# Turning a feed-forward pair with 64x64 identity products on the quarters of the array in place of 128x128 transposes

## The chip, the core and the metric

The kernel runs on one core of a Trainium2 chip. The metric is the device time of one execution in microseconds. Besides it there is a profile of one execution, with the start and the length of every instruction on TensorE (PE, with its weight loads as PEld), VectorE (DVE), ScalarE (ACT), GpSimd (POOL) and of the DMA queue of SyncE (SP).

## The reference, cut to what matters

Layer 0 works on `x` of four batches, 512 time steps, 128 x 64 features; layer 1 is a filter over time by Fourier modes. All is float32. The change sits where layer 0 ends, in the store of its output:

```python
to = layernorm(jnp.swapaxes(to, 1, 2), time_ln_g, time_ln_b)
x = x + to.reshape(b, t, f, h)
mid = jax.nn.gelu(x @ ffn_W1 + ffn_b1)      # 64 -> 256
x = x + (mid @ ffn_W2 + ffn_b2)             # 256 -> 64
...
x = _L1_conv_ref(x, w_real, w_imag)         # layer 1
```

## The kernel before

Layer 0 keeps the data feature-major: a chunk is 128 features (two groups of 64) on the partitions and 512 times along the free axis. 64 chunks make one batch; they are worked in 32 pairs. Layer 1 reads the data time-major from DRAM (`x4`), so each pair has to be turned before it is stored. In every second pair the two groups of 64 stand exchanged (the list HALVES does this on the host).

The stages of layer 0 are generators that a hand-written order (`in_turn`) advances by shares, two at a time; TensorE's order is exactly the order in which they issue (`tc.manual_schedule`). The other engines' queues are filled by a planner, which places each instruction by the times that it works out itself, except where `keep_in_program_order` pins it. The stages are: `project` (L412, keys, values and receptance), `scan`, `attend_and_convolve`, `convolve_time` with its taps (L632 on ScalarE, L636 on VectorE) and sums (`add_up`, L250), `open_feed`, and `feed_forward`. A part of the next batch's time convolution is made ahead inside `feed_forward` of batches 0 and 1 (`convolve_ahead`; `normed` gives L624 and L627 on VectorE, `tapped` gives L632 and L636).

`feed_forward` of batches 0 and 1 stands beside `project` of batches 2 and 3, that of batch 2 beside `convolve_time` of batch 3, that of batch 3 alone. I call them passes 0 to 3. Pass by pass, for each pair:

- `store` turns the pair finished one or two pairs before: eight transposes (L781) into one of two PSUM pairs of banks, `m` and `c`, which `unit()` hands out in turn. ScalarE copies the banks to `ob`, in pairs of even number with one instruction (L794), in pairs of odd number with two, which set the exchanged groups right (L789). Behind the second of these a GpSimd DMA writes `ob` (L790).
- `widen` is issued four times (L745: four products of 64x64 weights, one on each quarter of the array, each in two passes), each time into the next bank pair of `unit()`; ScalarE makes the gelu, `mid` (L750).
- `narrow` comes after each `widen` (L760) and sums in two further banks; after the fourth, VectorE adds the residual (L773) and makes `x4t`.
- `residual` (L704, L705 on VectorE) and `add_residual` (L713 on ScalarE, L716 on VectorE) prepare the pair after the next.

So one block of TensorE is: project or sums if any, turn, then widen and narrow four times by turns. The lines that set a float32 turn are:

```python
pt = unit()
for j, x4t in enumerate(x4s.pop(i)):
    for t in range(NT):
        nc.tensor.transpose(pt[:, j, t * P : (t + 1) * P], x4t[:, t * P : (t + 1) * P], ident)
```

Of the kernel before, what the change touches and what calls it, by code (L numbers as in the profile page):

```python
# [16 lines left out]
P = 128  # L17
T = 512
NF = 128
H = 64  # L20
# [5 lines left out]
NT = T // P  # L26
# [54 lines left out]
def layer0(ctx, tc, dram, x, xt, vecs, wkvr, wo, wdec, wconv, fbias, w1, fb1, w2, fb2, x4):  # L81
# [4 lines left out]
    nc = tc.nc  # L86
# [19 lines left out]
    def two(pool, tag):  # L106
        return pool.tile([P, 2, SL], F32, tag=tag, name=tag)


    ident = const.tile([P, P], F32, name="ident")  # L110
# [51 lines left out]
    halves = [slice(0, H), slice(H, P)]  # L162
# [133 lines left out]
    def spare(tag, n):  # L296
        if tag in ("wk", "wx"):
            return wxp.tile([P, 2, n], F32, tag=tag, name=tag, bufs=2 if tag == "wk" else 3)
        return fr.tile([P, 2, n], F32, tag=tag, name=tag, bufs=4 if tag == "z" else 3)

    def c_bank():
        return two(ps_c, "c")
# [4 lines left out]
    def of_p():  # L307
        return ps_p.tile([P, SL], F32, tag="p", name="p")
# [336 lines left out]
    def convolve_ahead(b, bank):  # L645


        rb, mb = yield from rows(bank, *carried[b], "rm3")
        ahead[b] = rb, mb
        for i in range(AHEAD):  # L650
            xr = spare("x1", SL)
            normed(b, i, xr, xr, rb, mb, True)
            yield
            tapped(b, i, xr, spare("z", SL), True)
            yield
# [43 lines left out]
    def residual(b, i):  # L699
        rb, mb = scale[b]  # L700
        x2 = fetch("kx", x2d, b, i)
        to = fetch("kh", tod, b, i)
        d = two(bk, "kd")
        nc.vector.tensor_tensor(d, to, pair_of(rb), ALU.mult)  # L704
        nc.vector.tensor_tensor(d, d, pair_of(mb), ALU.subtract)  # L705
        return x2, d

    def add_residual(b, i, x2, d):
        x3 = spare("z", SL) if b == B - 1 and i < 2 else bk.tile([P, 2, SL], F32, tag="k3", name="x3", bufs=3)
        for j in range(2):  # L710
            c = slice(2 * i + j, 2 * i + j + 1)

            tc.keep_in_program_order(nc.scalar.activation(  # L713
                d[:, j, :], d[:, j, :], AF.Identity, bias=vec[:, B4, c], scale=vec[:, G4, c]
            ))
        nc.vector.tensor_tensor(x3, d, x2, ALU.add)  # L716
        return x3
# [9 lines left out]
    def feed_forward(b):  # L727
        x3s = opened.pop(b)
        mids, x4s, obs, sums2 = {}, {}, {}, {}
        lag = 1 if b + 2 < B else 2  # L730
        turn = [0]
        while not free_s[0]:
            yield BLOCKED
        feeding[0] = True

        def unit():
            turn[0] ^= 1
            return two(ps_m, "m") if turn[0] else c_bank()

        def widen(i, q):  # L740
            x3 = x3s[i]
            pm = unit()
            for h in range(2):
                for j in range(2):
                    nc.tensor.matmul(  # L745
                        pm[halves[j], h, :], lhsT=w1_sb[halves[h], q * H : (q + 1) * H], rhs=x3[halves[h], j, :],
                        start=True, stop=True,
                    )
            mid = mids[i, q] = bk.tile([P, 2, SL], F32, tag="mid", name="mid", bufs=4)
            gelu = nc.scalar.activation(mid, pm, AF.Gelu_apprx_tanh, bias=fb1_sb[:, q : q + 1])  # L750
            if i == NPR - 3:
                after["scalar"] = gelu.ins

        def narrow(i, q):
            if q == 0:
                sums2[i] = of_p(), ps_s.tile([P, SL], F32, tag="s", name="pb")
            mid = mids.pop((i, q))
            for h in range(2):
                for j in range(2):
                    nc.tensor.matmul(  # L760
                        sums2[i][j][halves[h], :], lhsT=w2_sb[halves[j], q, :], rhs=mid[halves[j], h, :],
                        start=q == 0, stop=q == 3,
                    )
            if q < 3:
                return
            x3 = x3s.pop(i)
            if lag > 1:
                pair = spare("wx", SL)
                x4s[i] = [pair[:, j, :] for j in range(2)]
            else:  # L770
                x4s[i] = [bk.tile([P, SL], F32, tag="x4t", name="x4t", bufs=3) for _ in range(2)]
            for j, pa in enumerate(sums2.pop(i)):
                summed = nc.vector.scalar_tensor_tensor(x4s[i][j], pa, fb2_sb, x3[:, j, :], ALU.add, ALU.add)  # L773
            if i == NPR - 3:
                after["vector"] = summed.ins

        def store(i):
            pt = unit()
            for j, x4t in enumerate(x4s.pop(i)):
                for t in range(NT):  # L780
                    nc.tensor.transpose(pt[:, j, t * P : (t + 1) * P], x4t[:, t * P : (t + 1) * P], ident)  # L781
            s = i // 2
            if i % 2 == 0:
                obs[s] = bk.tile([P, NT, SL], F32, tag="ob", name="ob")
            o = obs[s][:, :, i % 2 * 2 * P : (i % 2 + 1) * 2 * P].rearrange("p t (j w) -> p j t w", j=2)
            pt = pt.rearrange("p j (t w) -> p j t w", t=NT)
            if i % 2:
                for h in range(2):
                    nc.scalar.copy(o[:, :, :, halves[1 - h]], pt[:, :, :, halves[h]])  # L789
                nc.gpsimd.dma_start(  # L790
                    x4[b][:, s * SL : (s + 1) * SL].rearrange("(t p) d -> p t d", p=P), obs.pop(s)
                )
            else:
                nc.scalar.copy(o, pt)  # L794

        early = None
        done = 0.0
        quarter = 2.25 * (NPR + 1) / (NPR + lag)
        widen(0, 0)
        widen(0, 1)  # L800
        for i in range(NPR + lag):
            if i >= lag:
                store(i - lag)
            for q in range(4):
                done += quarter
                if i < NPR:
                    if q < 2:
                        widen(i, q + 2)
                    elif i + 1 < NPR:
                        widen(i + 1, q - 2)  # L810
                    if i + 2 < NPR and q == 1:
                        coming = residual(b, i + 2)
                        if b == B - 1 and i % 4 == 2:
                            after["sync"].append(last_fetch[0].ins)
                    if i + 2 < NPR and q == 3:
                        x3s[i + 2] = add_residual(b, i + 2, *coming)
                    narrow(i, q)
                if q == 3 and b + 2 < B and i > 1:
                    early = early or convolve_ahead(b + 1, lambda: unit()[:, 0, :])
                    next(early, None)  # L820
                if q == 3 or narrowly:
                    yield done
                    done = 0.0
        feeding[0] = False
# [400 lines left out]
```

## Time and profile before

| | |
|---|---|
| time, median of 3 runs | 3683.86 us (3683.42 to 3687.7) |
| the profiled execution | 3685.27 us |
| its span, first to last instruction | 3683.5 us |
| mean granted TensorE clock | 0.985 |
| busy: PE, PEld, DVE, ACT, POOL | 94%, 37%, 73%, 48%, 12% |
| L781, all turns | 1024 transposes, 133.7 us of PE |
| pass 0, 820 to 1200 us | PE 97%, DVE 73%, ACT 63% |
| pass 1, 1470 to 1850 us | PE 97%, DVE 73%, ACT 63% |
| pass 2, 2110 to 2450 us | PE 91%, DVE 91%, ACT 84% |
| pass 3, 2450 to 2722 us | PE 98%, DVE 60%, ACT 80% |
| layer 1, from 2722 us | PE 96% |

A row of a timeline gives the start in us from the span's start, the length in us, the engine, the line, the operation, what it writes and reads, the shape, and how many instructions were joined. The bracket at its end is the idle time of the engine ahead of it and what ended that. A row of the waits names the waiting engine and line, whom it waited for, and us in total, times, and the longest. Float32 products show as two passes each, transposes as one. PE's ends are modelled, its starts are not.

### The profile page before, as it was taken

Reading aid. Unit: us, or ns where it says so; the run is one execution under the profiler, and the core shown is the slowest. Engines: PE = TensorE matmul, PEld = TensorE weight load, DVE = VectorE, ACT = ScalarE, POOL = GpSimd, SP = SyncE. Lnnn points to the kernel's source line nnn. Section 1 sums busy time; section 2 is a strip of 40 time slices with the busy share of each in tenths; the row PEclk is TensorE's granted clock in tenths of the full one; section 3 lists DMA queues with packets and bytes.
Section 4 is the critical chain, followed back from the end, with each engine's and each line's share of the span. In section 5 each row is a group of like instructions: output and inputs, shape, how many; then the busy total and the mean of one; then the engine's idle time right before and its main releaser. Section 6 shows DMA issues by size and latency. Waiting matters only on the chain. (4 is left out here: it accounts for less than half of the span.)

```text
span 3683.5 us, 54528 instructions
## 1 busy us (share of the span) xinstructions
PE 3480.4 (94%) x20553; PEld 1372.7 (37%) x20553; DVE 2671.6 (73%) x3498; ACT 1778.1 (48%) x2331; POOL 448.4 (12%) x657
## 2 busy tenths in 40 slices
PE   8989998889999899999999989999999999999998
PEld 3433332224333223443322333333333833328433
DVE  4464469986777896677789799956677277892677
ACT  0013346556666565666656588878864200152100
POOL 0000012220111121011112121200000000001000
PEclk9999999999999999999999999999999999999999
DMA  9886647787885688888568777746668478994687
GB/s 302 284 269 211 204 164 269 255 277 264 294 288 183 237 279 280 277 289 292 172 239 284 239 238 256 238 173 218 225 194 277 154 245 293 308 290 161 209 298 261
DMA packets 427991, 910.58 MB, mean 247 GB/s; under 512 B 32976, under 2 KB 83920, under 8 KB 423632
## 3 DMA queue, kind: packets, MB, share of 16 engines
q1 hardware_dynamic: 354160, 637.18, 53.1%
q0 software_dynamic: 71680, 268.46, 20.3%
q8 instruction: 164, 2.69, 0.3%
q10 hardware_dynamic: 1888, 1.45, 0.1%
q14 instruction: 99, 0.81, 0.1%
HBM read 638.46 MB, written 268.50 MB: 246 GB/s over the span
## 5 line engine op out<-in xcount | busy, mean ns | idle before, releaser
L760 PE MATMUL p<-mid,w_sb 64*64 64x512 f32 x2048 | 549.3, 595 | 17.9 <-DVE wx L773 17.9
L760 PE MATMUL pb<-mid,w_sb 64*64 64x512 f32 x2048 | 533.2, 595 | 0.0
L750 ACT ACTIVATE mid<-m,fb_sb 128x1024 f32<-128x1024 f32 x256 | 284.8, 1113 | 93.0 <-PE m L745 91.6
L750 ACT ACTIVATE mid<-c,fb_sb 128x1024 f32<-128x1024 f32 x256 | 284.5, 1111 | 91.2 <-PE c L745 89.1
L745 PE MATMUL m<-x,w_sb 64*64 64x512 f32 x2016 | 283.3, 613 | 7.5 <-ACT ob L794 5.3
L745 PE MATMUL c<-x,w_sb 64*64 64x512 f32 x2016 | 276.9, 604 | 12.9 <-ACT mid L750 6.6
L760 PEld LDWEIGHTS p<-mid,w_sb 64*64 64x64 f32 x2048 | 153.7, 134 | 290.9 <-issue 261.0
L1071 ACT COPY two<-a 128x512 f32<-128x512 f32 x64 | 37.5, 586 | 426.3 <-PE a L1066 426.3
L412 PE MATMUL a<-xp,wx 128*128 128x512 f32 x512 | 235.2, 603 | 0.5 <-DVE me L267 0.5
L1094 PE MATMUL b<-xin,avg_sb 128*128 128x512 f32 x512 | 230.8, 593 | 3.3 <-DVE xin L1100 3.3
L1100 DVE TENSOR_TENSOR xin<-b,pm 128x512 f32<-128x512 f32 x256 | 159.0, 683 | 97.9 <-PE b L1097 82.9
L581 ACT ACTIVATE sq<-x 128x1024 f32<-128x1024 f32 x128 | 135.1, 1055 | 150.5 <-DVE x L576 150.4
L250 PE MATMUL st<-x,ones 128*32 128x512 f32 x512 | 183.9, 609 | 23.8 <-DVE x L576 23.7
L636 DVE SCALAR_TENSOR_TENSOR to<-kd,vec,to 128x511 f32<-128x511 f32 (+1 forms) x272 | 197.0, 743 | 11.5 <-ACT to L632 8.0
L713 ACT ACTIVATE kd<-kd,vec 128x512 f32<-128x512 f32 x256 | 192.7, 803 | 3.1 <-DVE kd L705 3.1
L538 DVE TENSOR_TENSOR x<-a,xp 128x1024 f32<-128x1024 f32 x128 | 156.1, 1219 | 48.1 <-PE a L534 45.5
L946 DVE COPY xf<-b 128x256 f32<-128x256 f32 x128 | 54.4, 425 | 178.9 <-PE b L1040 170.0
L636 DVE SCALAR_TENSOR_TENSOR z<-x,vec,z 128x511 f32<-128x511 f32 x240 | 175.6, 744 | 5.0 <-ACT z L632 3.6
L716 DVE TENSOR_TENSOR x<-kd,kx 128x1024 f32<-128x1024 f32 x126 | 154.0, 1223 | 33.5 <-ACT kd L713 33.5
L534 PE MATMUL a<-rst,wo_sb 64*64 64x512 f32 x1024 | 143.3, 630 | 27.4 <-DVE x L538 25.3
L773 DVE SCALAR_TENSOR_TENSOR x4t<-p,fb_sb,x 128x512 f32<-128x512 f32 x64 | 47.7, 746 | 160.0 <-PE pb L760 157.5
L704 DVE TENSOR_TENSOR kd<-kh,rm 128x1024 f32<-128x1024 f32 x128 | 155.6, 1219 | 6.8 <-ACT rm L284 4.6
(271 smaller groups left out, 6762.7 us busy)
## 6 DMA issues: line engine op xcount, KB each, us to landing
xp<-in_xt SPq DMA_DIRECT2D x256, 512.0 KB
kh<-to SPq DMA_DIRECT2D x156, 512.0 KB
x<-x POOLq DMA_DIRECT2D x128, 512.0 KB, 4.6
kx<-x SPq DMA_DIRECT2D x128, 512.0 KB
x<-ob POOLq DMA_DIRECT2D x64, 1024.0 KB, 8.1
xin<-x SPq DMA_DIRECT2D x64, 1024.0 KB
out<-xin POOLq DMA_DIRECT2D x64, 1024.0 KB, 6.3
x<-x SPq DMA_DIRECT2D x96, 512.0 KB
```

The costliest lines, as they stand in the source:

```text
L250: nc.tensor.matmul(st[32 * q : 32 * q + 32, :], lhsT=ones, rhs=src[:, j, :], start=first, stop=last,)
L412: nc.tensor.matmul(pa[:, k, :], lhsT=wq[:, j, k * P : (k + 1) * P], rhs=xp[:, j, :], start=first and j == 0, stop=last and j == 1,)
L538: nc.vector.tensor_tensor(x1, at, xp, ALU.add)
L636: tap = nc.vector.scalar_tensor_tensor(to[:, j, k:], xr[:, j, : SL - k], vec[:, w, c], to[:, j, k:], ALU.mult, ALU.add)
L704: nc.vector.tensor_tensor(d, to, pair_of(rb), ALU.mult)
L713: tc.keep_in_program_order(nc.scalar.activation(d[:, j, :], d[:, j, :], AF.Identity, bias=vec[:, B4, c], scale=vec[:, G4, c]))
L716: nc.vector.tensor_tensor(x3, d, x2, ALU.add)
L745: nc.tensor.matmul(pm[halves[j], h, :], lhsT=w1_sb[halves[h], q * H : (q + 1) * H], rhs=x3[halves[h], j, :], start=True, stop=True,)
L750: gelu = nc.scalar.activation(mid, pm, AF.Gelu_apprx_tanh, bias=fb1_sb[:, q : q + 1])
L760: nc.tensor.matmul(sums2[i][j][halves[h], :], lhsT=w2_sb[halves[j], q, :], rhs=mid[halves[j], h, :], start=q == 0, stop=q == 3,)
L1094: nc.tensor.matmul(po[j], lhsT=avg_sb[:, j, :], rhs=xin[:, j, :], start=True, stop=False)
L1100: nc.vector.tensor_tensor(by_n(xin[:, j, :]), by_n(po[j]), by_c(pm[j % 2][:, j // 2, :]), ALU.add)
```

## The change

The eight transposes of a pair become 32 products. Of each 128 x 128 square of `x4t`, the four 64 x 64 quarters are loaded as weights, each on the quarter of the array that its rows (features) and its output partitions (times) name, and multiplied by the 64 x 64 identity, which moves through. The feature halves go to two banks: bank `h` holds rows `h` of both chunks. The copies read the banks in that new order; in pairs of odd number each of the two copies now reads one bank alone.

```diff
         def store(i):
             pt = unit()
+            pt = pt.rearrange("p h (t j w) -> p h t j w", t=NT, j=2)
             for j, x4t in enumerate(x4s.pop(i)):
                 for t in range(NT):
-                    nc.tensor.transpose(pt[:, j, t * P : (t + 1) * P], x4t[:, t * P : (t + 1) * P], ident)
+                    for h, rows in enumerate(halves):
+                        for k, at in enumerate(halves):
+                            tt = slice(t * P + k * H, t * P + (k + 1) * H)
+                            nc.tensor.matmul(
+                                pt[at, h, t, j, :], lhsT=x4t[rows, tt], rhs=ident[rows, rows], start=True, stop=True
+                            )
             s = i // 2
             if i % 2 == 0:
                 obs[s] = bk.tile([P, NT, SL], F32, tag="ob", name="ob")
-            o = obs[s][:, :, i % 2 * 2 * P : (i % 2 + 1) * 2 * P].rearrange("p t (j w) -> p j t w", j=2)
-            pt = pt.rearrange("p j (t w) -> p j t w", t=NT)
-            if i % 2:
+            o = obs[s][:, :, i % 2 * 2 * P : (i % 2 + 1) * 2 * P].rearrange("p t (j h w) -> p h t j w", j=2, h=2)
+            if i % 2 == 0:
+                nc.scalar.copy(o, pt)
+            else:
                 for h in range(2):
-                    nc.scalar.copy(o[:, :, :, halves[1 - h]], pt[:, :, :, halves[h]])
+                    nc.scalar.copy(o[:, 1 - h], pt[:, h])
                 nc.gpsimd.dma_start(
                     x4[b][:, s * SL : (s + 1) * SL].rearrange("(t p) d -> p t d", p=P), obs.pop(s)
                 )
-            else:
-                nc.scalar.copy(o, pt)
```

## The prediction

> **What bounds the kernel now.** I first read the busy shares: TensorE 94% of 3683.5 us, VectorE 73%, ScalarE 48%. The cheap conclusion, "TensorE bounds it, so a cheaper turn is a gain", needs a check by stage, because `store` runs only in the four feed-forward passes. The table of stretches gives them: passes 0 and 1 (820 to 1200 and 1470 to 1850 us) have TensorE busy 97%; pass 2 (2110 to 2450 us) is at 91% on TensorE and 91% on VectorE; pass 3 (2450 to 2722 us) at 98% on TensorE. A pass works in blocks, one per pair of feature chunks: TensorE issues other work (projection L412 in passes 0 and 1, sums L250 in pass 2, nothing in pass 3), then the turn L781, then four times widen (L745) and narrow (L760). The turn fills one of the bank pairs m and c. Widen 1 takes the other, widen 2 needs the turn's pair back (ScalarE's copy, L794 or L789), widen 3 needs the gelu of widen 1 (L750, "mid").
>
> So in each pass I look at what widens 2 and 3 wait for. The timelines of ScalarE and TensorE in a block of pass 0, times in us from the span's start, duration, then the wait:
>
> ```profile
> 984.31 1.04 PE L781 MATMUL m<-ident,x4t 128*128 128x128 f32 x8
> ...
> 985.27 1.09 PE L745 MATMUL c<-x,w_sb 64*64 64x512 f32 x8
> 985.38 1.01 ACT L794 COPY ob<-m 128x1024 f32<-128x1024 f32 x1 [2.75 <-PE m L781]
> ...
> 987.38 0.81 ACT L632 ACTIVATE z<-x,vec 128x512 f32<-128x512 f32 x1 [0.98 <-DVE x L627]
> ...
> 988.10 1.09 ACT L750 ACTIVATE mid<-c,fb_sb 128x1024 f32<-128x1024 f32 x1
> ...
> 989.10 0.81 ACT L632 ACTIVATE z<-x,vec 128x512 f32<-128x512 f32 x1
> ...
> 989.25 1.09 PE L745 MATMUL c<-x,w_sb 64*64 64x512 f32 x8 [0.31 <-ACT mid L750]
> ```
>
> ScalarE's gelu of widen 1 was ready to run at 986.4, but stands behind a tap activation (L632) that waits for VectorE; it ends at 989.19, and widen 3 starts 0.05 later. That 0.31 us is TensorE's only wait in the block, and it comes 9 times in each of passes 0 and 1.
>
> The waits of TensorE in pass 2, and two stretches of it (TensorE, weight loads, VectorE, ScalarE, GpSimd busy):
>
> ```profile
> PE p L760 <- DVE wx L773: 17.9, 6, 5.9
> PE c L745 <- ACT ob L789: 6.3, 11, 0.6
> PE m L745 <- ACT ob L794: 4.6, 9, 0.6
> ...
> 2160.00:2180.00 20.00, 18.95 (x165) 6.54 (x168) 19.79 (x23) 18.26 (x22) 3.64 (x5) 1.00 0.81 278
> ...
> 2280.00:2300.00 20.00, 18.95 (x168) 6.46 (x164) 19.83 (x23) 18.25 (x22) 3.99 (x5) 1.00 0.83 265
> ```
>
> Here VectorE is 99% busy, and in 20 blocks widen 2 already waits about 0.5 us for the turn's copy; about every fifth block TensorE waits some 2 us for VectorE.
>
> Pass 3, TensorE, its weight loads and ScalarE:
>
> ```profile
> 2573.76 1.09 PE L781 MATMUL m<-ident,wx 128*128 128x128 f32 x8
> 2574.78 1.09 PE L745 MATMUL c<-x,w_sb 64*64 64x512 f32 x8
> ...
> 2576.57 0.21 PEld L745 LDWEIGHTS m<-x,w_sb 64*64 64x64 f32 x8 [0.72 <-ACT ob L794]
> ...
> 2574.11 1.51 ACT L713 ACTIVATE kd<-kd,vec 128x512 f32<-128x512 f32 x2
> 2575.52 0.99 ACT L794 COPY ob<-m 128x1024 f32<-128x1024 f32 x1
> ```
>
> The copy stands behind two L713, these behind the gelu of widen 4. It ends at 2576.51, widen 2 starts 0.05 us later. So pass 3, though TensorE shows 98%, runs on a loop: widen 4, gelu, two L713, copy, widen 2. The turn is not in it.
>
> **What the Trainium skill says.** TensorEngine Tiling, Key Properties: changing the tiling mode drains TensorE. The trace agrees: from the last pass of L760 (0.43 us long) to L781 and from L781 to L745 about 0.1 us is lost each time (2565.05+0.43 to 2565.58; turns start to start 0.109, yet eight of them and the way to L745 take 0.96), and the first pass of L745 takes 0.05 more (1.09 against 1.04). TensorE: Matmul & The Clock Gate, LDWEIGHTS: a load is charged by its columns, so 64 cost half of 128; no row shows a steady run of them on four quarters. The same page, "Wait — 56ns, not 53.3ns?": starts never come closer than about 25 ns, however small the product; the trace starts passes on different quarters 0.01 apart, so this is only my upper bound. The same page, Architectural detail: ScalarE and VectorE are strict FIFO; the two fences above on passes 0 and 3 show just that.
>
> **The change part by part.** (a) Per turn, 8 transposes in one pass each (starts 0.109 us apart) go, and 32 products in two passes each come: 64 passes, 16 rounds if four quarters run at once, as L745 does (8 passes of 0.43 in 0.86). A round is bounded below by 64 moving columns, 64/512 of 0.43, or 0.054. The nearest row is L194, 64x64 weights with 16 columns on two quarters: four rounds in 0.41 us, of which 0.21 is the last one's length, so 0.20/3.1, about 0.06. I take 0.06: 0.96 us a turn; ends 0.90 (0.056 a round) and, as an estimate from the page's 25 ns a pass, 1.6.
> (b) The drains. By the product ahead, in the order of the trace, there are 126 runs of turns (two of them of two turns). 56 follow 128-row products (L412 and few others): before 0.96+0.05, after 0.09+0.96, so +0.04. 43 follow L760: before 0.11+1.02+0.05, after 0.96, so -0.22. 27 follow L250 (another mode): -0.13. If all of it counted: 56x0.04 - 43x0.22 - 27x0.13 = -11 us. But it doesn't: some 30 of the 43 lie in pass 3, whose loop leaves the turn out: 0. The 27 are in pass 2, where widen 2 waits for ScalarE anyway: 0, but for some five at its end. In passes 0 and 1 only the blocks with no wait count, about 34 x 0.04 = +1.4. The dozen mode changes at the ends of passes give -2. Sum of (a) and (b): -1.
> (c) The copies (L794: one of 1.0 us; L789: two of 0.59). L794 now writes runs of 64 where it wrote 128; L789 already did, and pays 586 ns for 512 columns, as the plain copy L1071 does (586). So 0; at most 0.05 x 64, outside pass 3 hidden. Their DMA (L790) is the same; two are issued two GpSimd instructions later, with 24 us to spare: 0. 0.9 MB more instructions to fetch beside 910 MB: 0.
> (d) **What moves.** ScalarE's order isn't written by hand; a planner places it, and I compared the orders of the two built programs. In passes 0 and 1, 18 blocks had copy, L632, gelu, L632, gelu; now copy, L632, L632, gelu, gelu. Four blocks had L632, copy, L632, gelu; now both L632 stand ahead of the copy. In pass 2 nearly every block's second L632 goes from behind the copy to before it. VectorE, GpSimd and SP keep their orders, but for seven L636 one place earlier and four GpSimd exchanges; TensorE's own is fixed. An L632 in the row costs ScalarE 0.72 us (987.38 to 988.10).
> Passes 0 and 1: the first L632 still starts at 987.38 (it waits for VectorE, whose chain starts at the end of the last narrow, not at the turn). The second now takes 988.10 to 988.81, the gelu ends 989.90 rather than 989.19, widen 3 starts 0.71 later. Behind the waiting L632 stand four gelus and two L713 on ScalarE; widen 3 waits for the first gelu, and narrow 3 behind it. Narrows and widens follow in order on TensorE, with no later wait to give it back, and the next block's VectorE chain starts from that narrow. In the four other blocks the copy and widen 2 come 0.71 later. 22 x 0.71 = +15.6.
> Pass 2: the loop gelu 4, L713, L713, L632, square, copy, widen 2 takes 9.8 us and grows by 0.71 in about 20 blocks; VectorE needs 10.0 in those, and some 2 us a cycle of five blocks is TensorE's wait for VectorE. So of 5 x 0.71 = 3.5 a cycle some 2 are absorbed; 1.5 x 4.6 cycles: +7. Ends: 0 and 24 x 0.71 = 17.
> Sum: -1 + 15.6 + 7 = +21.6. Against the profiled execution (3685.27 us; its span 3683.5 and 1.8 around it) that is 3706.9; against the median of 3683.86, 1.4 lower, 3705.5. I say **3705**.
>
> **Rivals.** *The drain pays* (faster): the L632 are covered after all, because the waits of L745 in passes 0 and 1 don't lengthen, and the full -11 of (b) comes: 3673. For it: some 110 drains go (two at each of the 43, one at each of the 27). Against: ScalarE's order is fixed and 0.05 us separates its ends from the starts of widens 2 and 3. It decides where an added wait is under 0.5 us in each of 22 blocks. 7%. *Cancelled*: part of the 15.6 is given back at the ends of passes 0 and 1 (there TensorE waits 1.9 us for a GpSimd power, L232, and 8.5 for L773) and pass 2 absorbs all: about 3689. 10%. *Quarters don't pack* (slower still): 1.6 us a turn; +0.6 in 34 blocks of passes 0 and 1, and +0.4 x 32 in pass 3, where the slack of the loop is then used up: +33 more, 3738. Against: L745 and L760 pack fully. 10%. The rest, 73%, is my forecast. That the change doesn't do what it says (transposes kept) is excluded by the built program, which has 4096 products of 64x64 and no transpose.
>
> **How the numbers follow.** A measurement of this kernel can tell about 0.2%, 7.4 us, from no change: 3676.5 to 3691.2. The forecast's own ends: pass 2 at 0 gives 3698, at 17 gives 3715. The range 3689 to 3722 takes in the cancelled case's middle and half of looser packing, and leaves out some 2 in 10. Faster 0.07, same 0.10, slower 0.83.
>
> **What would show it.** In the profile after: L632, L632, L750 in a row in passes 0 and 1, and the wait of L745 for mid 1.0 us in place of 0.31, 9 times a pass; pass 2 with waits for the copies near 1.2 us; pass 3 as long as before, with TensorE's wait ahead of widen 2 grown by 0.2; turns of 0.96 us. If pass 3 is shorter by 7 us, (b) is wrong; if passes 0 and 1 are not 7 to 8 us longer each, (d) is.

## The result and the profile after

| | before | after |
|---|---|---|
| time, median of 4 runs | 3683.64 us (3679.46 to 3687.7) | 3700.74 us (3695.82 to 3703.18) |
| span of the profiled execution | 3683.5 us | 3697.5 us (3699.32 in all) |
| TensorE busy | 3480.4 us | 3470.3 us |
| ScalarE's copies of the turns, mean | 1002 and 584 ns | 1002 and 584 ns |

The kernel became slower: ratio 1.0036, 95% interval 1.0021 to 1.0051. TensorE is busy 10 us less and the kernel takes 17 us more by the medians (8 to 19 by the interval).

Where the time lies is read best from ScalarE's copies of the even blocks, 16 in a pass, one fixed point in every second block. From the start of the first to the start of the last of a pass (us):

| | pass 0 | pass 1 | pass 2 | pass 3 |
|---|---|---|---|---|
| before | 364.3 | 362.7 | 316.5 | 242.1 |
| after | 369.9 | 370.0 | 320.7 | 241.7 |
| difference | +5.6 | +7.3 | +4.3 | -0.3 |

Together +16.9, about the difference of the medians. The other stretches (start-up, ends of passes, layer 1) differ by up to 13 us from kernel to kernel in the profiles of this study without following the edit, so they are left alone.

Two of the differences need a caution, because single profiles also differ in TensorE's granted clock. The trace shows it halved in stretches of 3.4 us. In pass 0 the profile before has two such stretches, at 1140 and 1168 us; pass 1, and both passes of the kernel after, have one each. The one at 1140 is the additional one, and it costs 1.6 us: the span between two even copies in which it lies takes 26.68 us in pass 0 and 25.08 in pass 1. Without it pass 0 grew by 7.2. Pass 2 is taken up again below.

The turn first. Line numbers after: L781 is now L785, L794 is L793, L789 is L796; lines up to L776 keep theirs. TensorE's timeline in a block of pass 3 of the kernel after:

```profile
2585.09 1.11 PE L785 MATMUL m<-ident,wx 64*64 64x64 f32 x64
2586.03 1.04 PE L745 MATMUL c<-x,w_sb 64*64 64x512 f32 x8
...
2587.33 0.60 PE L760 MATMUL pb<-mid,w_sb 64*64 64x512 f32 x2
2588.02 1.09 PE L745 MATMUL m<-x,w_sb 64*64 64x512 f32 x8
```

The turn of 64 passes takes 0.94 us up to the start of widen 1, which follows with no gap; its row is 1.04 long, not 1.09. At the end of the excerpt, widen 2 starts 0.69 us after the last row of the narrow ahead of it (2587.33 to 2588.02). Ahead of the later widens of the block the same distance is 0.42. The difference of 0.27 us is the wait for the copy, and the one place where TensorE stands still in the block.

Now ScalarE's timeline in a block of pass 0, the kernel after:

```profile
1009.56 1.01 ACT L793 COPY ob<-m 128x1024 f32<-128x1024 f32 x1 [3.00 <-PE m L785]
1011.31 1.52 ACT L632 ACTIVATE z<-x,vec 128x512 f32<-128x512 f32 x2 [0.73 <-DVE x L627]
1012.73 1.09 ACT L750 ACTIVATE mid<-c,fb_sb 128x1024 f32<-128x1024 f32 x1
```

and TensorE's in the same block:

```profile
1009.31 1.04 PE L745 MATMUL c<-x,w_sb 64*64 64x512 f32 x8
...
1013.88 1.09 PE L745 MATMUL c<-x,w_sb 64*64 64x512 f32 x8 [0.95 <-ACT mid L750]
```

The two L632 now stand in a row ahead of the first gelu, which ends 4.5 us after widen 1 began, where it was 3.9 before; widen 3 waits 0.95 us in place of 0.31. The waits of TensorE in one round of pass 0 (870 to 1140 us), after:

```profile
PE c L745 <- ACT mid L750: 8.4, 9, 1.0
PE m L745 <- ACT ob L793: 1.6, 2, 0.8
```

They were 2.6 and 0.4 us before. One more wait changed: once in each of passes 0 and 1 TensorE waits for a GpSimd power (L232), 1.9 us before and 1.2 after. And in pass 2 (2120 to 2465 us), after:

```profile
PE p L760 <- DVE wx L773: 16.0, 9, 5.8
PE c L745 <- ACT ob L796: 12.8, 11, 1.6
PE m L745 <- ACT ob L793: 9.6, 9, 1.4
```

Widen 2's waits for the copies, 6.3 and 4.6 before, have doubled; the wait for VectorE's sums fell only from 17.9 to 16.0. The granted clock changed as well. These are pass 2 of the kernel before, one of its stretches at half clock, and pass 2 of the kernel after; the third number from the end is the granted clock:

```profile
2136.00:2453.00 317.00, 291.69 (x2416) 110.52 (x2416) 285.50 (x324) 267.16 (x315) 59.71 (x77) 0.97 0.71 238
2259.90:2263.30 3.40, 3.40 (x22) 1.91 (x18) 3.40 (x5) 0.53 (x1) 0.00 (x0) 0.50 0.99 348
2145.00:2466.00 321.00, 288.20 (x4096) 112.29 (x4096) 284.92 (x323) 267.79 (x313) 74.80 (x77) 0.98 0.69 235
```

Before, the clock was halved for 20.5 us of pass 2, in stretches of which four begin about 1 us after the end of a wait of 1.9 to 2.2 us for L773, and 10.2 us of clock were lost. After, it was halved for 10.2 us, and 5.1 were lost.

### The profile page after: what moved, and what is told of

Its sections match the earlier page's. It is cut to its first block, busy times and chain, and to the rows that moved or that the text cites. A ratio compares the mean times of both kernels' runs of the same rounds, so it can differ in the third digit from the quotient of the medians.

```text
span 3697.5 us, 68871 instructions
## 1 busy us (share of the span) xinstructions
PE 3470.3 (94%) x27721; PEld 1384.9 (37%) x27721; DVE 2673.9 (72%) x3498; ACT 1777.9 (48%) x2331; POOL 462.9 (13%) x657
## 5 line engine op out<-in xcount | busy, mean ns | idle before, releaser
L760 PE MATMUL p<-mid,w_sb 64*64 64x512 f32 x2048 | 548.4, 594 | 16.0 <-DVE wx L773 16.0
L760 PE MATMUL pb<-mid,w_sb 64*64 64x512 f32 x2048 | 532.0, 594 | 0.0
L745 PE MATMUL c<-x,w_sb 64*64 64x512 f32 x2016 | 272.7, 598 | 32.2 <-ACT mid L750 17.3
L745 PE MATMUL m<-x,w_sb 64*64 64x512 f32 x2016 | 276.6, 604 | 16.0 <-ACT ob L793 12.9
L760 PEld LDWEIGHTS p<-mid,w_sb 64*64 64x64 f32 x2048 | 154.1, 134 | 284.4 <-issue 237.8
L412 PE MATMUL a<-xp,wx 128*128 128x512 f32 x512 | 236.3, 605 | 0.5 <-DVE me L267 0.5
L250 PE MATMUL st<-x,ones 128*32 128x512 f32 x512 | 183.7, 610 | 26.1 <-DVE x L576 26.0
L713 ACT ACTIVATE kd<-kd,vec 128x512 f32<-128x512 f32 x256 | 192.6, 802 | 3.1 <-DVE kd L705 3.1
L773 DVE SCALAR_TENSOR_TENSOR x4t<-p,fb_sb,x 128x512 f32<-128x512 f32 x64 | 48.0, 749 | 170.0 <-PE pb L760 167.4
L704 DVE TENSOR_TENSOR kd<-kh,rm 128x1024 f32<-128x1024 f32 x128 | 155.7, 1219 | 9.5 <-ACT rm L284 5.3
```

The source lines that it names most:

```text
L250: nc.tensor.matmul(st[32 * q : 32 * q + 32, :], lhsT=ones, rhs=src[:, j, :], start=first, stop=last,)
L412: nc.tensor.matmul(pa[:, k, :], lhsT=wq[:, j, k * P : (k + 1) * P], rhs=xp[:, j, :], start=first and j == 0, stop=last and j == 1,)
L713: tc.keep_in_program_order(nc.scalar.activation(d[:, j, :], d[:, j, :], AF.Identity, bias=vec[:, B4, c], scale=vec[:, G4, c]))
L745: nc.tensor.matmul(pm[halves[j], h, :], lhsT=w1_sb[halves[h], q * H : (q + 1) * H], rhs=x3[halves[h], j, :], start=True, stop=True,)
L760: nc.tensor.matmul(sums2[i][j][halves[h], :], lhsT=w2_sb[halves[j], q, :], rhs=mid[halves[j], h, :], start=q == 0, stop=q == 3,)
```

## The experiments

Two theories. **Order**: the loss is where the planner put the L632 on ScalarE, and the turn itself is worth next to nothing where it now stands. **Turn**: the products, their drains or the re-shaped copies cost the time. Each kernel's lines are shifted by its edit; the tile names tell which is which. The ratios are to the kernel before, measured beside each run.

### Products, old order

```diff
+    def order(z, ins):
+        follow(z, ins)
+    def placed(j, z, ahead_of):
+        if ahead_of is not None:
+            if j and ahead_of < 11:
+                order(z, copies[-1] if ahead_of in (3, 7) else gelus[-4])
+            return
...
+        if k in (9, 15, 21, 26):
+            order(z, gelus[-8])
+        elif j == 1 and k > 2:
+            order(z, copies[-1] if k in (7, 8, 13, 14, 19, 20, 24, 25, 30, 31) else copies[-2])
```

`follow` adds an edge of order alone between two instructions of ScalarE; `gelus` and `copies` hold those traced so far, `k` counts the taps of pass 2.

> The kernel after, with each second L632 activation pinned to the place on ScalarE that it has in the kernel before (behind the first gelu of its block in passes 0 and 1, behind the copy in pass 2), nothing else. Theory 1, the order is the loss: the +7.6, +7.6 and +4.4 us by which passes 0, 1 and 2 are longer in the kernel after go, so about 3701 - 19 = 3682 us, and L745 waits for mid near 0.3 us in pass 0 in place of 1.0. Theory 2, the turn itself is the loss (its products, their drains, or the form of the copy): the time stays at 3700 us, and the waits of L745 stay near 1.0.

Measured: 1.0001 of the kernel before (0.9991 to 1.0011); passes 363.1, 362.8, 316.0 and 241.7 us. (The expectation read the three differences as 7.6, 7.6 and 4.4; those of the table above are used here.) TensorE's wait for mid in pass 0, this run:

```profile
PE c L772 <- ACT mid L777: 2.0, 9, 0.2
```

The whole loss goes with the order. In the trace ScalarE's 2331 instructions stand in the order of the kernel before, without exception, and GpSimd's 657 in that of the kernel after; so GpSimd's few exchanges are not the cause. The same run says that the products, in the old order, gain nothing that the time shows.

Pass 2 is less certain than passes 0 and 1. Four of the runs below also have the products and the old order in pass 2, and it takes 317.3 to 318.4 us there. Two others (the turn twice, and the first try at pass 3) have the products and the new order: 318.7 and 318.8. The kernel after, with 320.7, is the longest of its kind, and this run the shortest of its own. By the means the order costs 2.1 us in pass 2, with 0.3 to 4.7 between single profiles. Passes 0 and 1 of these kernels repeat within 0.4 us where the order is the same.

### Transposes, new order

The same places, with the edge turned round (`follow(ins, z)`), on the kernel before.

> The kernel before, with its 128x128 transposes, and ScalarE's order of the kernel after (gelu or copy pinned behind the L632 activation that comes ahead of it there). Theory 1, the order is the loss: 3684 + 19 = 3703 us, with L745 waiting 1.0 us for mid 9 times in pass 0. Theory 2, the turn itself: 3684 us. In between, near 3693: the order hurts only together with the other turn.

Measured: 1.0049 (1.0037 to 1.0061); passes 369.2, 369.6, 319.1 and 242.0. TensorE's wait for mid in pass 0:

```profile
PE c L773 <- ACT mid L778: 7.9, 8, 1.0
```

The loss comes without the products (ScalarE's order is here that of the kernel after, but for one gelu). The theory of the turn falls, from both sides.

### Products, both L632 behind the second gelu

```diff
-            if j and ahead_of < 11:
-                order(z, copies[-1] if ahead_of in (3, 7) else gelus[-4])
+            if ahead_of < 11:
+                order(z, gelus[-3])
```

> Products with the old order in pass 2, and in passes 0 and 1 both L632 of a pair in a row again, but behind the second gelu of the block in place of ahead of the first. If it is the run of two (1.4 us against a slack of some 0.4 to 0.7) that delays a gelu, passes 0 and 1 are again about 370 us each and the whole 3687 + 14 = 3701 us, with TensorE waiting near 1.0 us for mid at another gelu. If it is the place right behind the copy that has no slack, passes 0 and 1 are near 363 us and the whole near 3687.

Measured: 0.9970 (0.9962 to 0.9977); passes 0 and 1 take 357.5 us each, better than before. ScalarE in a block of pass 0 of this run:

```profile
983.39 1.01 ACT L821 COPY ob<-m 128x1024 f32<-128x1024 f32 x1 [3.00 <-PE m L813]
984.31 1.11 ACT L777 ACTIVATE mid<-c,fb_sb 128x1024 f32<-128x1024 f32 x1
986.03 1.11 ACT L777 ACTIVATE mid<-m,fb_sb 128x1024 f32<-128x1024 f32 x1 [0.60 <-PE m L772]
987.04 1.51 ACT L657 ACTIVATE z<-x,vec 128x512 f32<-128x512 f32 x2
988.45 1.10 ACT L777 ACTIVATE mid<-c,fb_sb 128x1024 f32<-128x1024 f32 x1
```

The run of two does no harm here: no widen waits for a gelu any more, but for one of 0.5 us at the end of each pass. By then VectorE's L627 has long been done, so the 0.73 us of idle ScalarE goes as well, and the third gelu starts 2.42 us after the second, where the second followed the first after 1.72, without making TensorE wait. So it is not that two stand in a row but that they stand ahead of the first gelu, where one of them already cost a wait.

The gain is larger than either expectation, because a wait costs TensorE more than its row shows. In the old order the row gives 0.2 us, yet a pair of blocks with one such wait takes 23.61 us there and 23.18 here. The narrow ahead of widen 3 takes 1.23 us from its start to widen 3's in place of 0.86, and widen 3 itself 0.91 in place of 0.86: together 0.43. The idle time in a row is counted only from the modelled end of the product ahead (0.60 us after its start, where the next one follows after 0.43 if nothing holds it).

### The turn twice in pass 3

```diff
-                            nc.tensor.matmul(
+                            for _ in range(2 if b == B - 1 else 1):
+                                nc.tensor.matmul(
```

> The kernel after, with every one of the 64 products of a turn issued twice in pass 3 (the second overwrites the first with the same values), which makes 32 turns of 0.96 us about 0.9 us longer each. If the turn lies beside the loop in pass 3 (it ends 0.9 us before the copy that follows it can start, because ScalarE still has the two L713 to do), pass 3 stays at 241.7 us within 2 us and the wait of the second widen for the copy stays near 1.0. If the turn is on the loop, pass 3 grows by 30 x 0.9 = 27 us, to 3728 us in all.

Measured: 1.0082 (1.0069 to 1.0094); pass 3 260.8 us, +19.0, neither of the two. A block grew from 8.15 to 8.75 us, by 0.60, for a turn longer by 0.95. TensorE and ScalarE in a block of pass 3 of this run (the other 5 of the turn's 128 passes stand in rows of their own):

```profile
2598.35 2.08 PE L786 MATMUL c<-ident,wx 64*64 64x64 f32 x123
```

```profile
2598.93 1.51 ACT L713 ACTIVATE kd<-kd,vec 128x512 f32<-128x512 f32 x2
2600.58 1.07 ACT L798 COPY ob<-c 128x512 f32<-128x512 f32 x2
```

The turn now ends together with the two L713 (2600.43 and 2600.44), and the copy follows both. The first 0.35 us of the added turn are hidden, the rest shows: TensorE's own time in a block, without waits, is 4 x 1.716 + 0.94 = 7.80, and 7.80 + 0.95 = 8.75. The turn lay beside the loop, but only 0.35 us below it. My "1.0 us of wait" was misread. It is this row of TensorE's weight loads, in the kernel after:

```profile
2588.01 0.21 PEld L745 LDWEIGHTS m<-x,w_sb 64*64 64x64 f32 x8 [0.97 <-ACT ob L793]
```

The loads wait while TensorE still works on the narrow ahead; of the 0.97 us TensorE stood idle 0.27 (the timeline of pass 3 above), and 0.05 went into the longer row of the widen behind the wait.

### Pass 3 with the L713 elsewhere: four failures, then two that worked

The first try placed one L713 behind the second and one behind the third gelu, and fetched a block earlier.

```diff
+                    if apart and i + 2 < NPR and q in (1, 2):
+                        half_residual(i + 2, coming[1], q - 1)
+                        if q == 2:
+                            x3s[i + 2] = add_residual(b, i + 2, *coming, True)
+                            if i + 3 < NPR:
+                                coming = residual(b, i + 3)
```

> The kernel after; in pass 3 alone the two L713 activations of a block, which stand between its fourth gelu and the next copy, are placed one after the second and one after the third gelu, where ScalarE is idle 0.6 us each, and their operands are fetched a block earlier. If pass 3 is a loop in which the copy waits for gelu 4 and two L713, and the second widen waits for the copy (1.0 us of wait in each of 28 blocks), the wait nearly goes: 28 x 0.9 = -25, about 3676 us. If pass 3 is held by something else as well (the gelus, the fetches), under 5 us are gained: 3696 to 3701.

> The kernel before with the same move of the L713 in pass 3. Loop theory: the wait of 0.8 us in each of some 26 to 30 blocks goes, -20, about 3663 us. The turn of products is 0.2 us a turn shorter with what lies around it, and this was hidden in pass 3: if so, pass 3 of the run before this one (products, halves early) is about 6 us shorter than pass 3 of this run; if the products' turn is no shorter on TensorE's path, the two passes are equal.

Measured: 1.0275 (1.0262 to 1.0289) and 1.0238 (1.0225 to 1.0252); pass 3 326.3 and 324.9 us. Then the addition of the residual was pinned behind the sums traced ahead of it, and ScalarE's old order was put back in passes 0 to 2 of the products:

```diff
+        if halves_done:
+            tc.keep_in_program_order(whole)
```

> Products with ScalarE's old order in passes 0 to 2, and in pass 3 the two L713 early as before, with one thing mended: the addition of the residual is pinned on VectorE behind the two sums of the block before, which it overtook in the first try and held up (DVE waited 155.7 us for L710 in pass 3, and the sums came late). If the loop theory of pass 3 holds (copy behind gelu 4 and two L713, second widen behind the copy), the 28 waits of 1.0 us go to about 0.1: -25 against the products with the old order, 3688 - 25 = 3663 us. If another loop is as long (the gelus' own, VectorE's, the fetches), pass 3 stays near 241.7 us and the time near 3688.

> The kernel before with the same edit of pass 3, so that it differs from the run before this one by the turn alone. Loop theory: the 26 waits of 0.8 us go, -20: 3667 us. What the turn is worth where nothing hides it is read from pass 3 of the two: the prediction's 0.2 us a turn would make pass 3 of the products some 6 us shorter; no difference would mean that the shorter drains are worth nothing on TensorE's path either.

Measured: 1.0232 (1.0218 to 1.0247) and 1.0235 (1.0221 to 1.0249), pass 3 again 326.3 and 324.9. VectorE in a block of pass 3, products, and TensorE's wait over the pass:

```profile
2586.89 1.23 DVE L746 TENSOR_TENSOR x<-kd,kx 128x1024 f32<-128x1024 f32 x1 [7.38 <-ACT kd L737]
2588.15 1.23 DVE L731 TENSOR_TENSOR kd<-kh,rm 128x1024 f32<-128x1024 f32 x1
2589.41 1.23 DVE L732 TENSOR_TENSOR kd<-kd,rm 128x1024 f32<-128x1024 f32 x1
2590.56 0.74 DVE L806 SCALAR_TENSOR_TENSOR wx<-p,fb_sb,x 128x512 f32<-128x512 f32 x1
```

```profile
PE p L793 <- DVE wx L806: 51.7, 25, 2.1
```

VectorE has 7.4 us to spare and still is late: three residual instructions, 3.7 us, go off when the second L713 ends, just ahead of the sums (ready about 2587.5), and the next narrow needs the sums' bank. The Trainium skill (TensorE: Matmul & The Clock Gate, Architectural detail) calls VectorE strict FIFO; this is what it looks like. Earlier L713 set off earlier work, which collided with the sums. The pin on the addition moved nothing in pass 3: VectorE's order in a block, and its 155.7 us of waiting for the L713, are those of the first try, and the two scaling instructions still stand ahead of the sums. Not all of the longer pass is this wait: in both tries with products TensorE's clock was also halved in eight stretches of 3.4 us of pass 3, 13.7 us of clock, where the kernel after has none.

The third try has both L713 behind the second gelu, and the residual's scaling and addition pinned in program order, the scaling behind the sums:

```diff
+                    if apart and i + 2 < NPR and q == 1:
+                        x3s[i + 2] = add_residual(b, i + 2, *coming)
+                        if i + 3 < NPR:
+                            fetched = fetch("kx", x2d, b, i + 3), fetch("kh", tod, b, i + 3)
...
                     narrow(i, q)
+                    if apart and i + 3 < NPR and q == 3:
+                        coming = residual(b, i + 3, fetched)
```

> Products with ScalarE's old order in passes 0 to 2; in pass 3 both L713 stand right behind the second gelu, with operands fetched and scaled a block earlier, and VectorE's order is pinned so that the two sums of a block come ahead of the residual's work (in the two tries before, that work held the sums up by 3 us, and TensorE waited for the sums' bank). TensorE's own time in a block of pass 3 is 4 x 1.716 + 0.94 = 7.80 us against a block of 8.15, so not 1.0 but 0.35 us a block can be gained: 28 x 0.35 = -10, about 3677 us, pass 3 at 232 us. If the copies, the gelus or VectorE make another loop of 8.15, pass 3 stays at 241.7; if the sums are late again, it is longer.

> The kernel before with the same edit of pass 3. A turn behind a second product takes 1.54 us from the start of that product's last pass to the start of the next widen with transposes and 1.34 with products. If that gain was hidden in pass 3 by ScalarE's loop, it shows here: TensorE's block is 7.80 + 0.20 = 8.0, so pass 3 gains only 28 x 0.15 = -4 (237.5 us, 3683 in all) and the products' pass 3 is 5 to 6 us shorter than this one. If pass 3 is equally long in both, the gain of the shorter turn is not real on TensorE's path.

Measured: products 0.9971 (0.9962 to 0.9980), pass 3 232.3 us; transposes 1.0003 (0.9995 to 1.0011), pass 3 239.8. TensorE around a turn of pass 3, products:

```profile
2592.07 0.60 PE L791 MATMUL pb<-mid,w_sb 64*64 64x512 f32 x2
2592.49 1.11 PE L816 MATMUL c<-ident,wx 64*64 64x64 f32 x64
2593.42 1.04 PE L775 MATMUL m<-x,w_sb 64*64 64x512 f32 x8
2594.28 0.59 PE L791 MATMUL p<-mid,w_sb 64*64 64x512 f32 x2
```

and transposes:

```profile
2592.58 0.60 PE L763 MATMUL pb<-mid,w_sb 64*64 64x512 f32 x2
2593.11 1.09 PE L784 MATMUL c<-ident,wx 128*128 128x128 f32 x8
2594.13 1.09 PE L748 MATMUL m<-x,w_sb 64*64 64x512 f32 x8
2595.04 0.60 PE L763 MATMUL p<-mid,w_sb 64*64 64x512 f32 x2
```

Narrow to narrow 2.21 against 2.46 us: 0.25 a turn, 7.5 us in the pass. The expectation had 0.20, up to the start of widen 1; the 0.05 by which widen 1 is shorter behind products comes on top. The blocks take 7.80 and 8.05 us, and TensorE's rows show no wait in either. So the shorter turn is real, and in the kernel as changed pass 3 hides it.

### Both orders together

> Products, both L632 behind the second gelu in passes 0 and 1, the old order in pass 2, and in pass 3 the two L713 behind the second gelu. The two gains lie in different passes and should add: passes 0 and 1 at 357.5 us each (10.5 together against the products with the old order) and pass 3 at 232.3 (-9.4): 3687.5 - 20 = 3668 us.

> The same orders with the transposes: TensorE waits for nothing in the loops of passes 0, 1 and 3, so the turn alone decides there. A turn behind the 128-row products of passes 0 and 1 takes 1.396 us from the start of the last pass ahead of it to the next widen with transposes and 1.504 with products, 25 times a pass; behind a second product, in pass 3, 1.54 against 1.34. So passes 0 and 1 should be 2.7 us each shorter than with products (354.8 us) and pass 3 7.5 longer (239.8): 2 us slower in all than the run before this one, 3670 us. If passes 0 and 1 are equally long in both, the 0.108 us is hidden there by another engine even without these waits.

Measured: products 3665.12 us, 0.9942 of before (0.9925 to 0.9959), passes 357.5, 357.5, 317.6 and 232.3; transposes 3671.42 us, 0.9963 (0.9947 to 0.9980), passes 356.4, 356.7, 316.2 and 239.8. The gains add up. The products' version has the lowest median of all, though the intervals of the two overlap. In passes 0 and 1 the transposes are ahead by 0.06 us a turn (23.41 against 23.53 us a pair of blocks), half of what I expected: I had counted turns to the start of widen 1 and left out that behind a transpose widen 1 itself takes 0.05 longer, as the two fences above show.

## Why the prediction was right, step by step

- **(a), the turn**: 0.06 a round and 0.96 in all were taken. From its first pass to the next widen the turn took 0.98 us behind 128-row products (61 ns a round) and 0.93 behind L760 (58). The estimate of 1.6 from the skill's page (TensorE: Matmul & The Clock Gate, "Wait — 56ns, not 53.3ns?") does not hold for passes on four quarters: 64 in 0.93 to 0.98 us is 15 ns a pass.
- **(b), the drains**: +0.04, -0.22 and -0.13 a turn were taken. Counted to the end of widen 1, measured +0.06 behind L412 (0.108 to widen 1's start, less 0.05), -0.25 behind L760, -0.09 behind L250. The -11 in all stands as about -10, and that it would not show stands too: the products in the old order equal the kernel before within 0.1%, and pass 3 gave up its 7.5 us only when ScalarE's loop was cut. But the claim that the turn is simply not in that loop was too strong: with products TensorE's own 7.80 us are 0.35 from the loop's 8.15, and with transposes its 8.05 were only 0.10 from it.
- **(c), the copies**: 0 was taken, and the means are the same to the nanosecond.
- **(d), the order, passes 0 and 1**: this carried the forecast, and the step of 0.71 us a block is what the runs showed. Between the products in the old and in the new order a pair of blocks with one wait grew from 23.61 to 24.31 and from 23.66 to 24.36 us, 0.70 each. The wait of widen 3 grew by less against the kernel before, from 0.31 to 0.95, because the turn's own +0.06 behind 128-row products fills part of it. Where the sum was too large is the count. 22 blocks were to grow; 20 did, which is 14.0 us and not 15.6. In the eleventh block of each pass the 0.7 us is given back by the wait for L232, which fell from 1.9 to 1.2. The prediction's "no later wait to give it back" was wrong there.
- **(d), pass 2**: 7 us were taken, and about 2 were measured (0.3 to 4.7). The waits for the copies came as forecast, 22.4 us in 20 blocks or 1.1 each. What gives them back did not: some 9 us of TensorE's waits for VectorE were to go, and from the first to the last even copy they fell only from 14.1 to 12.3. On the other side stand 5.1 us less of lost clock. Whether the clock was granted because the long waits were broken up was not tried, so why pass 2 gave so much back stays open.
- **The rivals**: *the drain pays* needed L745's waits not to lengthen, and they did. *Cancelled* was right in part: about 1.4 us at L232 and most of pass 2. *Quarters don't pack* is excluded by the 0.98 us.
- The forecast's own test was 7 to 8 us for each of passes 0 and 1. The table has 5.6 and 7.3, and 7.2 and 7.3 without the additional stretch at half clock.
- The sum against the profiled execution, 3706.9, came out 7.6 high: 4.7 of it lies in the four passes (21.6 less 16.9), the rest in stretches that vary between runs.

Left open: why the planner put the L632 where it did (only its orders were forced, its reasons were not tried), and what the granted clock did to pass 2.

## What to carry to other kernels

When an edit touches an engine that a planner schedules, compare the built orders on the other engines first: here the edit was worth -10 us on TensorE, nothing in the time, and the order that came with it +16 to +17. Before crediting a wait as gain, compare the starts of the instructions with those of a block that does not wait. The wait of TensorE's weight loads (1.0 us in pass 3) was too large a measure, since 0.35 could be gained there, and the idle time in TensorE's own row (0.2 us in pass 0) too small, since 0.43 could. Put work that nobody waits for behind the instruction that someone does, and check what its results set off on the next engine.

## What the runs showed of the hardware

Sixty-four passes of 64 x 64 weights and 64 moving columns, spread over four quarters, ran at 58 ns a round of four between other 64-row products (0.93 us a turn) and showed no drain towards them; behind 128-row products the turn took 0.98 us and started 0.09 later. A turn of eight 128-row transposes between 64-row products took 0.25 us longer than the 64 passes, of which 0.05 stands in the row of the products that follow (1.09 for 1.04).
